# Four graph layers on one core: another fold in the convolution, hub blocks loaded earlier, messages kept in SBUF, a last chunk by tiles

## The chip, the cores and the metric

The kernel runs on one core of a Trainium2 chip, as one launch. The metric is the device time of that launch in microseconds. The engines are named as the profile names them: PE is TensorE's matrix products and PEld its weight loads, DVE is VectorE, ACT is ScalarE, POOL is GpSimd, and SP is SyncE, whose queue issues most of the DMAs.

## The reference

`x` has 8 graphs of 2048 nodes with 64 features, and `adj` (2048 x 2048, ones and zeros) is one graph's edges, shared by all eight. Node numbers near zero have many neighbours (the probability of an edge falls with the root of each end's number). Four layers follow one another, each as `x = x + layer(relu(layernorm(x)))`:

```python
# layer 0: attention over hyperedges, mixed with a product adj @ (x W_ind)
pair = jnp.stack([industry, g], axis=2)
coefs2 = softmax(tanh(pair @ fcW + fcb) @ av, axis=-1)
out = einsum('bnk,bnkf->bnf', coefs2, pair)

# layer 1: a Chebyshev graph convolution with weights of each node
w = einsum('nd,dkio->nkio', embedding, weight)      # K = 3 orders, 16 embedding numbers
As = [I, A, 2 A A - I]
x_g = einsum('knm,bmc->bnkc', stack(As), x)
out = einsum('bnki,nkio->bno', x_g, w) + b

# layer 2: three steps of message passing
for _ in range(3):
    effects = einsum('nm,bmd->bnd', adj, v)
    h = relu(concat([v, effects]) @ W1.T + b1)
    v = h @ W2.T + b2

# layer 3: graph attention over adj, softmax, h_prime + bias
```

So the adjacency is multiplied into something five times after layer 0: twice for the Chebyshev orders of layer 1, and once in each step of layer 2.

## The kernel before

**Layout.** The 2048 nodes are 16 tiles of 128 (`NT`), four tiles are a chunk of 512 (`TC`, `CW`), and there are four chunks (`NC`). The 8 x 64 features are four pairs q of 128 (`NP`: two graphs by 64 features). Tensors are held transposed, features on the partitions, in two `Halves`; slots of SBUF named `q0` to `q9` are handed from stage to stage by their names. Messages, with nodes on the partitions (128 x 512 a tile, 256 KB), go to DRAM as `sent[...]`.

**The product with adj.** For a target tile t the first three source tiles (`HUBS` = 3) are dense: six products of 128x512 from a copy in two parts (`Hub`, high and low). The other sources of t are a list of rows; each group of up to 128 is gathered from `sent` by an indirect DMA on POOL (`Feed.fetch`, L2578), split in two parts by ACT (L2595) and DVE (L2596), and multiplied with a 128x128 block of adj (`cells`). `LISTED` says how many groups a tile has: 7, 6, 5, 4 or 3. Target 0 is different: it takes all 13 other tiles whole (`FAR` = 13, blocks `zero`), which SP loads from `sent` (L2576). `Feed` keeps `raws` gathered tiles and splits `ahead` of the products; `group` is how many blocks of weights one cast on ACT covers. `Feed.own` loads the target's own message for the diagonal term, and `finish` makes z.

**The mixing (`mix`, L686).** The last stage of layer 0, chunk by chunk, with `Lists.fill` (L2472) beside it: 60 indirect DMAs bring blocks of adj and DVE masks them into `cells`.

**First product of layer 1 (`layer1_near`, L1624).** `Lists.load` (L2506) loads the three dense rows of blocks (1 MB each) and the 13 blocks of target 0, each cast on DVE to bf16. Then 16 targets; each result goes to DRAM as `sent[1]`.

**Convolution (`convolution_near`, L1679).** The second order is a product with adj again, made chunk by chunk by the generator `product(place)`, one chunk ahead of the convolution that uses it; `product(0)` runs alone before the convolution begins. The convolution of a chunk runs over the four pairs q and over blocks of the embedding, two at a time; for each block PE makes four products with `w01` (both first orders) into one of six PSUM banks `pk`, then, with `w2`, adds the second order; DVE multiplies the bank by the embedding's row (L1834), and POOL adds it to one of two accumulators `half` (L1840; the last block's add is DVE's). Each accumulator holds two halves of 64 partitions, of which the sum over halves is the result. `fold_up` lets PE add the halves with a stationary matrix `fold` into the bank `side`, and DVE adds that to x (L1736). `waiting` is a list of small pieces of work (fold, norm, store, messages) that are popped once after each pair of blocks (twice in the last chunk), and `advance()` spreads the pieces of the next product evenly over 30 places. Messages of the first step of layer 2 are made here in the last chunk; `send` (L1864) copies each from PSUM to `u` and stores it.

**Layer 2 (`layer2_near`, L1880).** Three steps of 16 targets. After each target, `turn` transposes z and applies ReLU, and `after` either makes the next step's message or, in step 2, at the end of each chunk, runs `chunk`: product with `w2`, residual, norm (`Scores.chunk`, L2726: centre, squares, root, reciprocal L287, write), the first products of layer 3, and their rows to DRAM (`f_rows`, L2753). Beside the steps a generator `neighbours` (L1975) sorts the lists for layer 3 with MAX8 and MATCH_REPLACE on DVE, one instruction per group of products. `Scores` is made at the start of layer 2, with its small loads and a product of `aa`.

**Layer 3** gathers from `f_rows` on POOL (L2819), and its result ends the kernel.

The order on each engine is that of the program as a scheduler moved it; engines run their own queue in order.

Of the kernel before, what the change touches and what calls it, by code (L numbers as in the profile page):

```python
# [19 lines left out]
P = 128  # L20
# [26 lines left out]
F16 = mybir.dt.float16  # L47

# [86 lines left out]
class Kernel:  # L135
# [1488 lines left out]
    def layer1_near(self, slots, k2, far):  # L1624
# [11 lines left out]
        with (  # L1636
# [3 lines left out]
            lists.load(w)  # L1640
# [38 lines left out]
    def convolution_near(self, slots, k):  # L1679
# [27 lines left out]
        fold = k.tile([P, D], F, name="fold")  # L1707
        nc.vector.tensor_add(fold, ident[:, lo], ident[:, hi])

        with (  # L1710
# [21 lines left out]
            def fold_up(q, accs):  # L1732
                po = side()
                for i, h in enumerate((lo, hi)):
                    self.mm(po[h], fold, accs[i])
                nc.vector.tensor_add(x[:, q], po, x[:, q])  # L1736

            def message(t):
                pn = steps.first_message(v, t, bank())
                self.send(0, t, pn, lists.hub, w)  # L1740

            feed = Feed(
                self, lists, w, self.sent[1], None, raws=4, casts=2, ahead=1, group=2,
# [3 lines left out]
            def product(place):  # L1747
                ch, aah = chunks[place], aahs[place % 2]

# [7 lines left out]
                for i in range(TC):  # L1757
                    t = ch * TC + i
                    own = feed.own(t)
                    acc = ps.tile([P, CW], F, name="acc")  # L1760
                    feed.dense(acc, t, lists.hub)
                    yield
                    for n, _ in enumerate(feed.listed(acc, t)):
                        if n == 1 and last is not None:
                            turn(*last)
                        yield
# [18 lines left out]
            def pieces(place):  # L1785
                targets = [chunks[place] * TC + i for i in range(TC)]
                return sum(2 + (LISTED[t] or FAR) for t in targets)

# [6 lines left out]
            for place, ch in enumerate(chunks):  # L1795
# [4 lines left out]
                many, hook = 0 if ends else pieces(place + 1), 0  # L1800

                def advance():
                    nonlocal hook
                    for _ in range(many * hook // 30, many * (hook + 1) // 30):
                        next(ahead, None)
                    hook += 1

                if ends:
                    for c in chunks[:-1]:
                        for t in range(c * TC, (c + 1) * TC):  # L1810
                            waiting.append(lambda t=t: message(t))
                for q in range(NP):
                    accs = [w.tile([P, CW], F, name="half", bufs=4) for _ in range(2)]
                    sides = list(enumerate(((xe, hi), (xo, lo))))
                    for blk in range(0, NBLK, 2):
# [7 lines left out]
                        advance()  # L1823
# [19 lines left out]
                        advance()  # L1843
                        if waiting:
                            waiting.pop(0)()
                    waiting[:0] = [lambda: None, lambda q=q, accs=accs: fold_up(q, accs)]
# [3 lines left out]
                norm = self.norm_parts(ch, x, Part(v, s), Part(u, s), std, bank, write)  # L1850
# [13 lines left out]
    def send(self, step, t, pn, hub, w, later=None):  # L1864

        nc = self.nc
        u = w.tile([P, CW], F, name="u", tag="z")
# [12 lines left out]
    def layer2_near(self, slots, k2):  # L1880
# [3 lines left out]
        with (  # L1884
# [9 lines left out]
            last = Scores(self, slots, k, w, ps)  # L1894
            accs, late = {}, []

            def messages(step, t):
                pn = ps.tile([P, NP, P], F, name="pn")
                for q in range(NP):
                    self.mm(pn[:, q], v(q)[:, t * P : (t + 1) * P], seen[step])  # L1900
                self.send(
                    step, t, pn.rearrange("n q f -> n (q f)"), hubs[step], w, later[:, 2]
# [22 lines left out]
            def chunk(ch):  # L1925
                s = slice(ch * CW, (ch + 1) * CW)
                x = last.x
                nc.sync.dma_start(x, self.xs[2][ch])
                for q in range(NP):
                    p2 = ps.tile([P, CW], F, name="p2")  # L1930
# [4 lines left out]
                self.store_x(2, ch, x)  # L1935
                last.chunk(ch)

            def after(step, t):
                if step < 2:
                    messages(step + 1, t)  # L1940
                elif t % TC == TC - 1:
                    chunk(t // TC)
# [4 lines left out]
            for step in range(3):  # L1947
# [3 lines left out]
                feed = Feed(self, lists, w, self.sent[2 + step], None)  # L1951
                for t in range(NT):
                    own = feed.own(t)
# [418 lines left out]
class Lists:  # L2372
# [99 lines left out]
    def fill(self, pool, w):  # L2472
# [3 lines left out]
        self.cells = pool.tile([P, PLACE[NT], P], BF, name="cells")  # L2476
# [8 lines left out]
        for c in range(0, PLACE[NT], group):  # L2485
# [8 lines left out]
            if len(late) > 2:  # L2494
                keep(*late.pop(0))
            yield
        for x in late:
            keep(*x)
        yield

    def open(self, pool):
        self.dense = pool.tile([P, HUBS, N], BF, name="dense")
        self.zero = pool.tile([P, FAR, P], BF, name="zero")
        self.hub = Hub(pool, "hub")

    def load(self, w):  # L2506

        nc, a = self.nc, self.kern.a
        for h in range(HUBS):
            raw = w.tile([P, N], F, name="dense_raw", bufs=1)  # L2510
            nc.sync.dma_start(raw, a["adjT"][h * P : (h + 1) * P])
            nc.vector.tensor_copy(self.dense[:, h], raw)
        raw = w.tile([P, FAR, P], F, name="zero_raw", bufs=1)
        nc.sync.dma_start(
            raw, a["adjT"][HUBS * P :, :P].rearrange("(i p) n -> p i n", p=P)
        )
        nc.vector.tensor_copy(self.zero, raw)
# [177 lines left out]
class Scores:  # L2695
# [3 lines left out]
    def __init__(self, kern, slots, k, w, ps):  # L2699
# [6 lines left out]
        self.sums = k.tile([P, NP, NC], F, name="sums")  # L2706
# [19 lines left out]
    def chunk(self, ch):  # L2726
        nc, kern = self.nc, self.kern

        def write(q, ch, xr, scale):
            nc.vector.scalar_tensor_tensor(  # L2730
                self.hn[:, q], xr, 1.0, scale, op0=OP.mult, op1=OP.mult,
                accum_out=self.sums[:, q, ch : ch + 1],
            )

        std = self.w.tile([P, CW], F, name="std", bufs=1)
# [394 lines left out]
```

## Time and profile before

The times are of nine runs; the profile is of one more execution. The mean clock granted to TensorE is a share of full speed.

| what | value |
|---|---|
| time, median of 9 runs | 1979.48 us |
| lowest and highest | 1972.14 and 1984.28 us |
| the profiled execution: its time | 1980.55 us |
| the profiled execution: span | 1978.8 us, mean clock 0.908 |
| PE busy | 1699.3 us, 86% |
| DVE busy | 1410.7 us, 71% |
| ACT busy | 810.8 us, 41% |
| POOL busy | 1035.3 us, 52% |
| gathers L2578 on POOL | 300, 1053 ns each |
| loads of own messages from `sent` (SP) | 52 of 256 KB, 4.2 us to landing |
| loads of whole messages for target 0 (SP) | 52 of 256 KB, 3.3 us to landing |
| stores of messages (SP) | 48 of 256 KB, 3.5 us to landing |

Stages in the profiled execution, in us from the start of the span: layer 0 to 621, of it the mixing from 479; the first product of layer 1 to 738; `product(0)` to 786; the convolution to 1253; its end, with norm and messages, to 1297; layer 2's steps to 1669, where step 0's last z is at 1406.92 and step 1's at 1528.34; the last chunk of layer 2 to 1702; layer 3 to the end. A row of a group gives the line, the engine, the operation, what it writes and reads, shapes and count; then its busy time and the mean of one in ns; then the idle time of the engine before it, and who ended that idle time.

### The profile page before, as it was taken

How to read it: one execution, taken by the hardware profiler on the slowest of the kernel's cores; microseconds unless marked ns; L12 is line 12 of the kernel's file. 1: busy time of each engine (PE TensorE's matmuls, PEld its weight loads, DVE VectorE, ACT ScalarE, POOL GpSimd, SP SyncE). 2: the span in 40 equal slices, each digit the busy share in tenths (PEclk: the TensorE clock that was granted, in tenths of full speed). 3: DMA queues.
4: the chain of work that ended last, by engine and by line, in shares of the span. 5: the costliest groups of instructions: out<-in, count | busy, mean ns of one | idle time of the engine just before them, and what ended most of it. 6: DMA issues, size and time to landing. Idle time of an engine off the chain costs nothing. (4 is left out here: it accounts for less than half of the span.)

```text
span 1978.8 us, 22332 instructions
## 1 busy us (share of the span) xinstructions
PE 1699.3 (86%) x7061; PEld 973.8 (49%) x7066; DVE 1410.7 (71%) x2389; ACT 810.8 (41%) x1627; POOL 1035.3 (52%) x959
## 2 busy tenths in 40 slices
PE   6859798998996787999999999769888899579885
PEld 2515666665323564444444444447667565345432
DVE  6777778885667674877677657588988576459774
ACT  5712354554664663222121010255666664257300
POOL 1100166666870753876765645266474641478770
PEclk8867899998996888999999989789989999789887
DMA  9740223344335776333131210368788774666665
GB/s 349 257 120 1 72 75 103 106 129 176 105 101 175 232 229 183 85 85 112 49 109 40 65 52 38 108 218 246 238 266 271 218 260 160 230 180 174 183 178 191
DMA packets 124057, 305.20 MB, mean 154 GB/s; under 512 B 29312, under 2 KB 31120, under 8 KB 118160
## 3 DMA queue, kind: packets, MB, share of 16 engines
q0 software_dynamic: 45328, 149.60, 25.1%
q1 hardware_dynamic: 76288, 149.80, 22.7%
q10 hardware_dynamic: 2304, 4.20, 0.6%
q8 instruction: 59, 0.97, 0.2%
q14 instruction: 78, 0.64, 0.1%
HBM read 240.40 MB, written 63.14 MB: 153 GB/s over the span
## 5 line engine op out<-in xcount | busy, mean ns | idle before, releaser
L2578 POOL DMA_INDIRECT raw<-sent,index x300 | 315.8, 1053 | 306.0 <-DVE part_lo L2596 119.9
L2596 DVE TENSOR_TENSOR part_lo<-raw,part_hi 128x512 fp32r<-128x512 f32 x352 | 265.6, 777 | 120.1 <-ACT part_hi L2595 106.0
L2595 ACT CAST part_hi<-raw 128x512 fp32r<-128x512 f32 x352 | 212.4, 619 | 314.8 <-PE acc L176 208.6
L1840 POOL TENSOR_TENSOR half<-half,y 128x512 f32<-128x512 f32 x192 | 247.3, 1317 | 133.9 <-DVE y L1834 128.7
L176 PE MATMUL pk<-q,w 128*128 128x512 f32 (+1 forms) x768 | 301.4, 610 | 2.4 <-DVE q L1724 0.9
L176 PE MATMUL acc<-q,ident 128*128 128x512 f32 x416 | 202.6, 613 | 24.6 <-DVE q L2909 18.2
L176 PE MATMUL acc<-part_hi,weights 128*128 128x512 f32 x365 | 176.0, 485 | 30.4 <-ACT part_hi L2595 30.0
L1834 DVE SCALAR_TENSOR_TENSOR y<-pk,bias,q 128x512 f32<-128x512 f32 x224 | 158.0, 742 | 52.2 <-PE pk L176 32.9
L176 PEld LDWEIGHTS pk<-q,w 128*128 128x128 f32 (+1 forms) x768 | 115.7, 190 | 155.9 <-issue 119.8
L176 PE MATMUL acc<-part_lo,weights 128*128 128x512 f32 x365 | 166.7, 458 | 24.5 <-DVE part_lo L2596 23.9
L2819 POOL DMA_INDIRECT ring<-f_rows,near x121 | 142.0, 1173 | 65.0 <-issue 28.9
L176 PEld LDWEIGHTS acc<-q,ident 128*128 128x128 f32 x416 | 76.9, 194 | 98.2 <-issue 43.0
L2305 POOL TENSOR_TENSOR q<-q,beta 128x512 f32<-128x512 f32 x57 | 76.1, 1337 | 72.4 <-DVE beta L2281 33.8
L176 PEld LDWEIGHTS acc<-part_hi,weights 128*128 128x128 f32 x365 | 74.2, 203 | 80.9 <-ACT part_hi L2595 46.9
L176 PEld LDWEIGHTS acc<-part_lo,weights 128*128 128x128 f32 x365 | 74.0, 203 | 72.7 <-DVE part_lo L2596 56.1
L176 PE MATMUL pp<-adj,x_ind_hi 128*128 128x512 f32 x256 | 89.3, 464 | 0.5 <-DVE q L846 0.3
L2564 ACT CAST hub_weights<-dense 128x384 fp32r<-128x384 bf16 x80 | 40.6, 511 | 101.4 <-PE acc L176 97.2
L2890 DVE TENSOR_TENSOR q<-ring,e 128x1024 f32<-128x1024 f32 x58 | 70.1, 1219 | 8.4 <-PE acc L176 8.2
L2305 POOL TENSOR_TENSOR q<-q,coef 128x512 f32<-128x512 f32 x57 | 63.1, 1108 | 20.9 <-DVE q L2328 17.6
L176 PE MATMUL pp<-adj,x_ind_lo 128*128 128x512 f32 x256 | 72.7, 404 | 0.0
L287 DVE RECIPROCAL std<-std 128x512 f32<-128x512 f32 x16 | 53.6, 3351 | 25.9 <-ACT std L286 21.9
L2489 POOL DMA_INDIRECT listed_raw<-in_adjT_dram,cell x60 | 62.9, 1048 | 16.5 <-issue 15.9
(503 smaller groups left out, 3427.6 us busy)
## 6 DMA issues: line engine op xcount, KB each, us to landing
rows<-in_adj_dram SPq DMA_DIRECT2D x16, 1024.0 KB, 9.1
adj_t<-in_adjT_dram SPq DMA_DIRECT2D x64, 256.0 KB, 3.0
own<-sent SPq DMA_DIRECT2D x52, 256.0 KB, 4.2
raw<-sent SPq DMA_DIRECT2D x52, 256.0 KB, 3.3
sent<-u SPq DMA_DIRECT2D x48, 256.0 KB, 3.5
q<-x SPq DMA_DIRECT2D x10, 1024.0 KB, 5.4
x<-q SPq DMA_DIRECT2D x9, 1024.0 KB, 3.9
links<-squares POOLq DMA_DIRECT2D x16, 512.0 KB, 8.2
```

Of the source, the lines that this page charges most:

```text
L176: self.nc.tensor.matmul(out, lhsT, rhs, start=start, stop=stop)
L287: nc.vector.reciprocal(std, std)
L1834: nc.vector.scalar_tensor_tensor(y, pks[b, half], bias[:, b : b + 1], emb[:, b], op0=OP.add, op1=OP.mult,)
L1840: add.tensor_add(acc, acc, y)
L2305: self.nc.gpsimd.tensor_tensor(x, x, by.unsqueeze(2).to_broadcast([P, NB, D]), op=OP.mult)
L2489: self.kern.behind(nc.gpsimd.indirect_dma_start(raw[:, i], None, rows, bass.IndirectOffsetOnAxis(ap=self.cell[:, c + i : c + i + 1], axis= ...
L2564: self.nc.scalar.copy(to, self.lists.dense[:, :, i * P : (i + 1) * P])
L2578: self.nc.gpsimd.indirect_dma_start(raw, None, self.rows[:], bass.IndirectOffsetOnAxis(ap=self.lists.index[:, c : c + 1], axis=0),)
L2595: nc.scalar.copy(hi, raw)
L2596: nc.vector.tensor_sub(lo, raw, hi.bitcast(F))
L2819: self.nc.gpsimd.indirect_dma_start(to, None, self.kern.f_rows[:], bass.IndirectOffsetOnAxis(ap=index, axis=0))
L2890: nc.vector.tensor_tensor(y.rearrange("n i (b f) -> n i b f", b=NB), block[:, i : i + 2, : NB * D].rearrange("n i (b f) -> n i b f", b=NB) ...
```

## The change

- The lists of blocks (`cells`, `dense`, `zero`) are held in unsigned 8-bit numbers, no longer in bf16. `Lists.load` is gone: `bring` loads the dense blocks and those of target 0 in 16 pieces (256 KB, the last one 64 KB) and casts each on DVE, one piece per step of `fill`, beside the mixing.
- `product(0)` takes four of the six `pk` banks as accumulators and makes all its hub products first. The feed of the convolution has `ahead` 3 for 1 and `group` 4 for 2; `own` has two buffers for one. `advance()` and its 30 places are gone: the next product goes on once for every second pair of blocks, a target being cut in two parts (target 0 in four).
- The sum of the halves: no `fold` product. `cross` copies the two half-accumulators that lie on the wrong partitions into `other` by two DMAs inside SBUF, and `fold_up` makes two adds of 64x512 and one of 128x512 on DVE, all in SBUF.
- In steps 0 and 1 of layer 2 the messages stay in SBUF (`kept`, the slots q2 and q3) as well as going to `sent`: `own` and the 13 tiles of target 0 are read from there. In the convolution's last chunk, the message of each chunk's last tile is made later than the others, and squares of the last norm lie in another buffer.
- The feed of layer 2 has `raws` 8 for 6 and `ahead` 4 for 2. `Scores` is made at the start of step 2.
- In step 2 the last four tiles go through `chunk` one at a time, 128 wide; x for layer 3 is stored in slices of the chunk.

```diff
@@ -1637,7 +1638,6 @@
-            lists.load(w)
             hub = Hub(w, "first_hub")
@@ -1729,23 +1726,39 @@
-            def fold_up(q, accs):
-                po = side()
+            def cross(accs):
+                other = w.tile([P, CW], F, name="other", bufs=1)
+                nc.sync.dma_start(other[lo], accs[0][hi])
+                nc.sync.dma_start(other[hi], accs[1][lo])
+                return other
+
+            def fold_up(q, accs, other):
                 for i, h in enumerate((lo, hi)):
-                    self.mm(po[h], fold, accs[i])
-                nc.vector.tensor_add(x[:, q], po, x[:, q])
+                    nc.vector.tensor_add(x[h, q], accs[i][h], x[h, q])
+                nc.vector.tensor_add(x[:, q], other, x[:, q])
+
+            kept = Halves(slots, "u", ("q2", "q3"), True)
 
             def message(t):
                 pn = steps.first_message(v, t, bank())
-                self.send(0, t, pn, lists.hub, w)
+                self.send(0, t, pn, lists.hub, kept(t))
 
             feed = Feed(
-                self, lists, w, self.sent[1], None, raws=4, casts=2, ahead=1, group=2,
+                self, lists, w, self.sent[1], None, raws=4, casts=2, ahead=3,
                 targets=[ch * TC + i for ch in chunks for i in range(TC)],
             )
 
             def product(place):
                 ch, aah = chunks[place], aahs[place % 2]
+                sums = {}
+
+                def begin(t):
+                    sums[t] = bank() if place == 0 else ps.tile([P, CW], F, name="acc")
+                    feed.dense(sums[t], t, lists.hub)
+
+                if place == 0:
+                    for i in range(TC):
+                        begin(ch * TC + i)
@@ -1757,13 +1770,15 @@
                     own = feed.own(t)
-                    acc = ps.tile([P, CW], F, name="acc")
-                    feed.dense(acc, t, lists.hub)
-                    yield
+                    if place > 0:
+                        begin(t)
+                    acc = sums.pop(t)
+                    stops = [LISTED[t] // 2 - 1] if t else [2, 6, 9]
                     for n, _ in enumerate(feed.listed(acc, t)):
-                        if n == 1 and last is not None:
+                        if n in stops:
+                            yield
+                        if n == stops[0] and last is not None:
                             turn(*last)
-                        yield
@@ -1797,17 +1808,9 @@
-                many, hook = 0 if ends else pieces(place + 1), 0
-
-                def advance():
-                    nonlocal hook
-                    for _ in range(many * hook // 30, many * (hook + 1) // 30):
-                        next(ahead, None)
-                    hook += 1
-
@@ -1820,7 +1823,8 @@
-                        advance()
+                        if blk % 4 == 0 or (q == 0 and chunks[(place + 1) % NC] == 0):
+                            next(ahead, None)
@@ -1840,14 +1844,19 @@
-                        advance()
                         if waiting:
                             waiting.pop(0)()
-                    waiting[:0] = [lambda: None, lambda q=q, accs=accs: fold_up(q, accs)]
+                    waiting[:0] = [
+                        lambda: None,
+                        lambda q=q, accs=accs, other=cross(accs): fold_up(q, accs, other),
+                    ]
+                    if ends and q < NP - 1:
+                        waiting.append(lambda t=q * TC + TC - 1: message(t))
@@ -1922,24 +1931,28 @@
-            def chunk(ch):
-                s = slice(ch * CW, (ch + 1) * CW)
-                x = last.x
-                nc.sync.dma_start(x, self.xs[2][ch])
+            def chunk(t, n):
+                ch, c = t // TC, t % TC * P
+                s = slice(t * P, t * P + n)
+                x = last.x[:, :, c : c + n]
+                if c == 0:
+                    nc.sync.dma_start(last.x, self.xs[2][ch])
...
             def after(step, t):
                 if step < 2:
                     messages(step + 1, t)
+                elif t >= NT - TC:
+                    chunk(t, P)
                 elif t % TC == TC - 1:
-                    chunk(t // TC)
+                    chunk(t - TC + 1, CW)
@@ -1948,9 +1961,12 @@
-                feed = Feed(self, lists, w, self.sent[2 + step], None)
+                    last = Scores(self, slots, k, w, ps)
+                feed = Feed(
+                    self, lists, w, self.sent[2 + step], kept if step < 2 else None, raws=8, ahead=4
+                )
                 for t in range(NT):
-                    own = feed.own(t)
+                    own = kept(t) if step < 2 else feed.own(t)
@@ -2473,7 +2489,10 @@
-        self.cells = pool.tile([P, PLACE[NT], P], BF, name="cells")
+        self.cells = pool.tile([P, PLACE[NT], P], U8, name="cells")
+        self.dense = pool.tile([P, HUBS, N], U8, name="dense")
+        self.zero = pool.tile([P, FAR, P], U8, name="zero")
+        dense = self.bring(w)
@@ -2493,28 +2512,41 @@
+            next(dense, None)
             yield
...
+    def bring(self, w):
+
+        for src, to in self.blocks():
+            raw = w.tile([P, 4, P], F, name="dense_raw", bufs=2)
+            raw = raw[:, : src.shape[1]] if len(src.shape) == 3 else (
+                raw.rearrange("p i n -> p (i n)")
+            )
+            self.nc.sync.dma_start(raw, src)
+            self.nc.vector.tensor_copy(to, raw)
+            yield
```

`Halves` is the class that the features already use: two tiles in named slots, here indexed by node tile.

## The prediction

> **What bounds the kernel now.** I read the busy times by stage first, since the page's chain of waits holds only 1% of the span and names nothing in the stages that the change touches. Columns: window, its length, then busy time of each engine with instruction count, the granted TensorE clock, DMA share, GB/s.
>
> ```profile
> core 0: us, PE busy (x) PEld busy (x) DVE busy (x) ACT busy (x) POOL busy (x), PEclk, DMA share, GB/s
> 479.00:621.00 142.00, 121.55 (x417) 40.56 (x415) 91.45 (x120) 77.23 (x107) 96.46 (x92) 0.89 0.40 128
> 738.00:786.00 48.00, 34.26 (x102) 20.35 (x103) 20.76 (x33) 18.71 (x40) 16.97 (x16) 0.77 0.66 197
> 786.00:1253.00 467.00, 459.17 (x1476) 196.92 (x1475) 327.26 (x433) 72.56 (x142) 293.51 (x240) 0.99 0.22 69
> 1253.00:1297.00 44.00, 32.20 (x116) 19.80 (x114) 25.20 (x42) 18.27 (x34) 5.89 (x6) 0.77 0.55 183
> 1297.00:1340.00 43.00, 29.02 (x144) 22.31 (x144) 36.65 (x52) 24.34 (x48) 28.51 (x27) 0.82 0.66 200
> 1340.00:1410.00 70.00, 65.87 (x391) 54.76 (x391) 63.33 (x83) 42.19 (x86) 39.54 (x37) 0.97 0.82 259
> 1410.00:1425.00 15.00, 10.92 (x46) 7.53 (x45) 14.73 (x19) 8.69 (x16) 4.80 (x4) 0.90 0.69 229
> 1425.00:1530.00 105.00, 92.10 (x504) 73.48 (x504) 88.81 (x119) 65.50 (x131) 68.52 (x65) 0.93 0.84 265
> 1530.00:1546.00 16.00, 13.99 (x64) 9.94 (x62) 12.28 (x19) 10.04 (x19) 4.72 (x5) 0.89 0.71 219
> 1546.00:1640.00 94.00, 88.79 (x426) 58.54 (x426) 63.35 (x112) 60.00 (x123) 52.19 (x52) 1.00 0.73 233
> ```
>
> The convolution (786 to 1253) is TensorE's: 459 of 467 us busy at a clock of 0.99, VectorE 327, GpSimd 294. The stretch before it, its own first product, is not: 34 busy of 48. In layer 2, PE and DVE are both nearly full in steps 0 and 1 (DVE 14.73 of 15 in the first change of step); step 2 is PE's.
>
> Then the groups of the convolution, shapes apart (count, busy us, mean ns, idle before and its releasers):
>
> ```profile
> L2596 DVE TENSOR_TENSOR part_lo<-raw,part_hi 128x512 fp32r<-128x512 f32 x55 | 68.5, 1256 | 31.2 <-ACT part_hi L2595 31.2
> L176 PE MATMUL side<-half,fold 128*64 128x512 f32 x62 | 17.6, 624 | 3.5 <-DVE half L1840 3.5
> L1736 DVE TENSOR_TENSOR q<-side,q 128x512 f32<-128x512 f32 x15 | 10.2, 678 | 0.0
> ```
>
> The product that folds two half accumulators is 17.6 us of a full engine. DVE's split L2596 takes 1256 ns here; the same shape in layer 2 takes 688:
>
> ```profile
> L2596 DVE TENSOR_TENSOR part_lo<-raw,part_hi 128x512 fp32r<-128x512 f32 x196 | 129.3, 688 | 45.8 <-ACT part_hi L2595 36.2 <-PE acc L176 7.8 <-ACT q L1920 1.0
> ```
>
> Last, single waits in the order of time (start, us, what, idle before in brackets), and the sum of waits over layer 2's steps (us, times, longest):
>
> ```profile
> 637.12 0.79 PE L176 MATMUL acc<-first_hub_h,hub_weights 128*128 128x512 f32 x1 [4.29 <-ACT hub_weights L2564]
> 741.51 0.94 POOL L2578 DMA_INDIRECT raw<-sent,index  x1 [11.46 <-PE acc L176]
> 748.45 0.62 ACT L2595 CAST part_hi<-raw 128x512 fp32r<-128x512 f32 x1 [5.37 <-DMA raw<-sent,index]
> 1290.10 1.01 POOL L2578 DMA_INDIRECT raw<-sent,index  x1 [34.18 <-DMA raw<-sent]
> POOL raw L2578 <- DMA raw<-sent: 30.4, 2, 20.0
> ```
>
> Gathers at the start of layer 2 wait for plain loads of the messages that target 0 needs in full; so they do at both changes of step.
>
> **The change, part by part.** All against the profiled execution, 1980.55 us (span 1978.8), 1.1 above the median of the runs shown.
>
> A, hub blocks in the mixing. Removed after 621: three casts L2512 of 1.23 and one of 1.02 on DVE, and SP's 1 MB loads between the stores; PE's first hub product waits 4.29 at 637. Gain 4.29, up to 10 if the first gather (643.81) follows: I take −6. Added in the mixing: 16 loads of 256 KB and 16 casts to 8 bits. That cast is in no row; bounds are a quarter of the 1.23 cast (0.31) and the 0.69 of other 128x512 passes, so 5 to 11 us of DVE. In the built order they stand in the first one and a half chunks of the mixing, where DVE is 20 to 21 busy of 35 us. Each waits at DVE's head for its landing (3.0 us in the row of the 256 KB adj_t loads), with L759 to L761 queued behind, which PE's products of the mixing await. Two buffers hide about half. If the 14 idle us per 35 cover all, 0; otherwise 12. I take +6. A together: 0 (−10 to +12).
>
> B, first product. Gathers take 1.25 us apart when not held (741.51, 742.76, 744.01); before, they are held by split buffers up to 6.8 us, and one accumulator serialises the four targets until 786. Four banks put all 24 hub products ahead of the data, and splits go four deep. Sixteen gathers × 1.25 = 20 us from 741.5, plus 7 from issue to first split, plus 4 for last split, products, z and turn: 772 to 774 instead of 786: −13 (−8 to −16, the latter if all follow A's earlier start).
>
> C, convolution. Off PE: −17.6, and of the 3.5 us idle ahead of it nothing counted. Onto DVE: three adds with both inputs in SBUF for one of 0.68, 16 times: 3 × 0.69 − 0.68 = 1.4 alone, or 3 × 1.256 − 0.68 = 3.1 at the stretch the split shows; 22 to 50 us of DVE, hidden by its 140 idle. If that cover is gone, up to +50 less the 17.6. Onto SP: 32 copies of 128 KB inside SBUF; the nearest row is 3.3 us for 256 KB. They wait at SP's head for the halves, with own rows, messages' stores and embedding loads behind; the add stands two hooks (some 11 us) later, so nothing waits, save after the last quarter: there copy 3.3 + adds 2.1 stand for products 1.3 + add 0.7, +3.4. The thirty small interruptions become eight lumps per chunk; I give them +1. C: −13 (−21 to +8).
>
> The Trainium skill, "SBUF — State Buffer", section "Who interferes with whom", speaks against the three adds: a VectorE instruction with both inputs in SBUF and a GpSimd instruction that reads SBUF exclude each other for whole instructions. The row agrees in kind (1256 against 688). By the rule at its worst each add waits out one GpSimd add of 1.317 us, 16 × 3 × 1.32 = 63 us of DVE, still under its 140 idle, so the time would be the same; by the row it is 27.
>
> D, messages kept on chip. At layer 2's start 13 loads L2576 issued over 1277.5 to 1289.1 go; the last message's store is issued by 1274.35 and takes 3.5, so gathers can begin at 1278 instead of 1290. DVE and PE have room (25 and 32 of 44), yet t=0 must still be split 13 times: −9 (−5 to −12). The small loads for the scores and PE's 3.49 wait on them move to step 2, hidden by PE's queue of ready products; no gain counted.
>
> At the changes of step, z of target 15 to z of target 0 takes 18.5 (1406.92 to 1425.40) and 17.3. Loads vanish there, and splits go four deep in place of two (E). But DVE is full there with the neighbour sort (MAX8 2.29, MATCH_REPLACE 2.27), and a wait removed only brings its next work forward. Over 1297 to 1546 DVE is busy 215.8 of 249 and PE 211.9: no more than 33 can go. The fullest long stretch now has PE at 94% (65.87 of 70), so I take half: −16 (0 to −30). Step 2 is at 88.79 of 94: −2 (0 to −5). DMA share there is 0.82 to 0.84, and 52 own and raw loads fewer only help.
>
> F, last chunk by tiles. Today's tail from the last z (1669.24) to the first gather of layer 3 (1702.01) is 33 us: turn 2.0, product p with its add to 1676, centring and squares to 1680.4, root to 1682.3, reciprocal 3.35, back and writes to 1692, four tiles' stores to 1699.5, then 2.5. At a quarter of the wide parts the last tile's own chain is 2.0 + 1.2 + 1.1 + 1.2 + 0.8 + 1.6 + 1.9 + 2.5 = 12.3; the tiles that queue before it after the last listed product, a chain and a half at some 8, make it 25. But all four have serial links on PE's in-order queue: small products waiting for ACT and DVE stop listed products behind them. Tail −8, stalls +5: −3 (−8 to +6).
>
> Sum: 0 − 13 − 13 − 9 − 16 − 2 − 3 = −56: 1924.5, less 1.1 for the median: 1923.
>
> **Rivals.** R1: layer 2 is DVE's. The sort and the splits only close ranks; the changes of step, deeper splits and tiles give nothing: −13 −13 −9 = −35, 1944. For it: 14.73 of 15 at the first change, 36.65 of 43 at the start. Against: 16 us of DVE idle in 1425 to 1530, and part_hi waiting for DMA 41.6 us.
>
> R2: the convolution turns to DVE/GpSimd locally; −13 becomes +5: 1941. For: the stretch above. Against: 140 idle us.
>
> R3, slower: the lumps. Three products ahead × 8 lumps; each brings up to four gathers in a row on GpSimd, which holds them until split buffers come free (longest 4.7 us in the convolution now, 38.8 in 26 waits), and its adds of y queue behind; y has three buffers, so DVE stops, then the six banks fill and PE stops. At 24 × 3 = 72 us the time is 1995. It decides from 24 × 2.6 = 62, my 56 and the 6 that tell a difference. Against: six banks hold one and a half pairs of blocks, each pair 5.6 us of PE, more than the longest hold.
>
> R4: it does not do what it says: loads in the mixing hold DVE for 3.0 + 0.69 each without overlap, 59 us in all, while the rest gains: 1923 + 53 = 1976. Against: the order has them in pairs with two buffers.
>
> **How the numbers follow.** Forecast 0.52, R1 0.22, R2 0.10, R3 0.08, R4 0.03, and 0.05 that more is won in layer 2 (33 of 33, below 1905). About 6 us (0.3%) can be told from none. Faster: all but R3, nearly all of R4 and an edge of R2: 0.88; within: 0.03; slower: 0.09. The forecast's own range is 1900 to 1946, its terms' half-widths combined; 1892 to 1958 takes in R1, R2 and some of the deeper gain, and leaves out R3 and R4.
>
> **What would show it.** A: first hub product near 630 and DVE waits on dense loads in 479 to 560 of some 6 us. B: from the first gather to the convolution's steady state about 32 instead of 45. C: no side<-half rows, PE still 97% busy, the stretch 13 shorter; L1737-like adds of 0.7 to 1.3. R3 shows as PE idle by DVE y in lumps. D: first gather of layer 2 some 4 us after the last store. E: changes of step near 12 to 14, DVE over 92%; if DVE is at 88% and the changes still 17, R1. F: last z to first gather near 25. The forecast is wrong if GpSimd, with gathers and adds in one queue, sets the pace anywhere in 786 to 1253.

## The result, and the profile after

The changed kernel takes 2002.6 us (median of 10 runs, 1988.85 to 2009.95); beside it the kernel before has 1978.07 (31 runs). The ratio is 1.011, with an interval from 1.009 to 1.013: slower by some 22 us, where 56 less were forecast. Run again in a later call it was 1.0121 (1.0089 to 1.0152).

The profiled execution of the changed kernel has a span of 2000.0, 21.2 above that of before. Cut at events that both kernels have, the difference lies as follows (us; "again" are profiles of the same two kernels from one later call):

| stage, from event to event | before | after | difference | before again | after again |
|---|---|---|---|---|---|
| start to the mixing's reciprocal at 556 (before) | 556.4 | 563.1 | +6.7 | 550.9 | 560.6 |
| to the last target of the first product, stored on its way | 181.6 | 178.3 | -3.3 | 184.4 | 177.1 |
| product(0), to its last z | 45.7 | 36.8 | -8.9 | 45.9 | 38.2 |
| convolution, to the reciprocal of its last chunk | 476.4 | 490.1 | +13.7 | 476.6 | 489.5 |
| to layer 2's first z | 37.3 | 25.5 | -11.8 | 38.2 | 25.1 |
| step 0, to its last z | 109.6 | 112.6 | +3.0 | 105.7 | 112.9 |
| step 1 | 121.4 | 121.3 | -0.1 | 123.2 | 123.0 |
| step 2, to the z of target 14 | 131.1 | 134.9 | +3.8 | 131.5 | 136.5 |
| to the z of target 15 | 9.8 | 15.7 | +5.9 | 9.8 | 15.7 |
| to layer 3's first gather | 32.8 | 40.3 | +7.6 | 33.2 | 40.1 |
| layer 3 | 276.8 | 281.4 | +4.6 | 279.1 | 276.7 |

The signs repeat in the second pair, except in layer 3, whose own code is the same in both kernels; step 1, which the change does touch, took the same time in both pairs. Two stages lost what the sum wanted to gain: the convolution, and the end of layer 2.

The windows of the changed kernel, which answer to those of before (window, length, then busy time and count of each engine, clock, DMA share, GB/s):

```profile
core 0: us, PE busy (x) PEld busy (x) DVE busy (x) ACT busy (x) POOL busy (x), PEclk, DMA share, GB/s
479.00:628.00 149.00, 122.84 (x410) 41.13 (x411) 95.41 (x129) 78.79 (x110) 92.51 (x90) 0.86 0.41 130
742.00:780.00 38.00, 31.26 (x105) 20.72 (x106) 20.00 (x32) 19.47 (x36) 16.56 (x16) 0.81 0.82 245
780.00:1262.00 482.00, 452.02 (x1413) 194.34 (x1411) 344.99 (x467) 69.02 (x129) 285.96 (x239) 0.98 0.25 75
...
1340.00:1406.00 66.00, 57.79 (x340) 49.16 (x340) 61.81 (x81) 38.31 (x78) 39.71 (x32) 0.95 0.59 178
1406.00:1425.00 19.00, 15.32 (x80) 11.46 (x78) 16.72 (x23) 11.32 (x24) 7.07 (x8) 0.92 0.43 133
1425.00:1528.00 103.00, 87.00 (x488) 73.85 (x489) 87.94 (x118) 63.49 (x129) 68.68 (x62) 0.93 0.81 254
1528.00:1548.00 20.00, 16.36 (x81) 12.46 (x80) 13.98 (x25) 11.18 (x22) 5.76 (x5) 0.92 0.49 144
```

In the convolution PE has less to do (452 busy) and yet the stage is longer: its idle time grew from 8 us in 467 to 30 in 482. In step 0 DVE is now busy 61.81 of 66, more densely than PE. The rows at 1406 and 1528 are the two changes of step: z of target 15 to z of target 0 takes 17.9 and 18.5 now, 18.5 and 17.3 before.

Groups of the convolution (count, busy, mean ns of one, idle before and its releasers) show who holds PE up. The first line is the kernel before, the others are the changed kernel:

```profile
L176 PE MATMUL pk<-q,w 128*128 128x512 f32 x500 | 231.7, 603 | 2.0 <-DVE q L1724 0.9 <-DVE y L1834 0.7
...
L177 PE MATMUL pk<-q,w 128*128 128x512 f32 x502 | 242.8, 620 | 23.1 <-DVE half L1838 10.8 <-DVE y L1838 8.1 <-DVE q L1721 2.1
...
L1737 DVE TENSOR_TENSOR q<-half,q 64x512 f32<-64x512 f32 x32 | 21.8, 681 | 0.5
...
L1738 DVE TENSOR_TENSOR q<-other,q 128x512 f32<-128x512 f32 x15 | 10.9, 726 | 21.7 <-DMA other<-half 19.8 <-issue 1.8
```

PE's products into `pk` waited 2.0 us in all before, 23.1 now, for banks that DVE has not read. And DVE stands 19.8 us for the copies of the fold. One quarter in order of time (start, us, what, idle before):

```profile
813.67 0.52 SPq L1731 DMA_DIRECT2D other<-half  x1
...
814.17 1.40 DVE L1737 TENSOR_TENSOR q<-half,q 64x512 f32<-64x512 f32 x2
814.28 0.56 SPq L1732 DMA_DIRECT2D other<-half  x1
818.19 0.69 DVE L1738 TENSOR_TENSOR q<-other,q 128x512 f32<-128x512 f32 x1 [2.62 <-DMA other<-half]
...
820.01 0.74 DVE L1838 SCALAR_TENSOR_TENSOR half<-pk,bias,q 128x512 f32<-128x512 f32 x1
...
820.81 9.18 PE L177 MATMUL pk<-q,w 128*128 128x512 f32 x20 [3.07 <-DVE half L1838]
```

The copies are issued at 813.7 and 814.3; the add that needs them is DVE's next work but one, and waits 2.62 us; behind it queue two splits and the next pair's first multiplication, and PE waits 3.07 for that. The program writes this add eight multiplications later. The scheduler had moved it up, and the order of the built kernel already said so.

The waits of layer 2's steps (us, times, longest) have lost the row of target 0's plain loads, and the first two that remain are about as large as before. The first two lines are the kernel before, the others the changed kernel, both from 1300 to 1640:

```profile
POOL raw L2578 <- DVE part_lo L2596: 56.9, 43, 6.8
ACT part_hi L2595 <- DMA raw<-sent,index: 41.6, 44, 2.9
...
POOL raw L2610 <- DVE part_lo L2628: 53.7, 22, 27.0
ACT part_hi L2627 <- DMA raw<-sent,index: 47.3, 46, 3.1
```

At the end of layer 2 the chains by tiles run one after the other (timelines, cut to the steps that repeat; the first line is the one wide reciprocal of the kernel before, the others are the changed kernel):

```profile
1682.31 3.35 DVE L287 RECIPROCAL std<-std 128x512 f32<-128x512 f32 x1 [1.96 <-ACT std L286]
...
1678.31 0.73 DVE L2671 SCALAR_TENSOR_TENSOR z<-own,self_weight,acc 128x512 f32<-128x512 f32 x1
...
1682.85 0.95 DVE L288 RECIPROCAL std<-std 128x128 f32<-128x128 f32 x1 [1.11 <-ACT std L287]
...
1688.39 2.30 PE L177 MATMUL p<-q,w 128*128 128x128 f32 x8
...
1694.35 0.95 DVE L288 RECIPROCAL std<-std 128x128 f32<-128x128 f32 x1 [1.02 <-ACT std L287]
...
1700.20 2.30 PE L177 MATMUL p<-q,w 128*128 128x128 f32 x8
...
1706.69 0.95 DVE L288 RECIPROCAL std<-std 128x128 f32<-128x128 f32 x1 [1.25 <-ACT std L287]
...
1718.66 0.94 POOL L2857 DMA_INDIRECT ring<-f_rows,near  x1 [15.43 <-DVE own L2963]
```

The reciprocals of tiles 13, 14 and 15 lie 11.5 and 12.3 us apart. A tile's first products `p` stand in PE's queue behind the last products of the tile before, so nothing of one chain covers the other. The 512-wide chain had one reciprocal of 3.35; three of 0.95 are no longer, but the waits from one engine to the next, such as DVE's 1.02 to 1.25 us in front of each reciprocal, are paid three times after the last z.

### The profile page after: what moved, and what is told of

The parts are those of the page before. It is cut to its first block, busy times and chain, and to the rows that moved or that the text cites. A ratio compares the mean times of both kernels' runs of the same rounds, so it can differ in the third digit from the quotient of the medians.

```text
span 2000.0 us, 22470 instructions
## 1 busy us (share of the span) xinstructions
PE 1688.5 (84%) x7093; PEld 982.0 (49%) x7098; DVE 1431.0 (72%) x2477; ACT 808.0 (40%) x1629; POOL 1036.0 (52%) x959
## 3 DMA queue, kind: packets, MB, share of 16 engines
q1 hardware_dynamic: 74672, 140.37, 21.2%
## 5 line engine op out<-in xcount | busy, mean ns | idle before, releaser
L2610 POOL DMA_INDIRECT raw<-sent,index x300 | 325.1, 1084 | 300.2 <-DVE part_lo L2628 148.1
L177 PE MATMUL pk<-q,w 128*128 128x512 f32 (+1 forms) x768 | 310.7, 623 | 23.1 <-DVE half L1838 10.8
L2628 DVE TENSOR_TENSOR part_lo<-raw,part_hi 128x512 fp32r<-128x512 f32 x326 | 244.1, 776 | 87.7 <-ACT part_hi L2627 81.9
L1844 POOL TENSOR_TENSOR half<-half,y 128x512 f32<-128x512 f32 x192 | 241.1, 1284 | 119.3 <-DVE y L1838 118.3
L2627 ACT CAST part_hi<-raw 128x512 fp32r<-128x512 f32 x326 | 195.4, 619 | 195.5 <-DMA raw<-sent,index 88.1
L177 PE MATMUL acc<-part_hi,weights 128*128 128x512 f32 x349 | 156.5, 450 | 26.1 <-ACT part_hi L2627 25.5
L177 PE MATMUL acc<-part_lo,weights 128*128 128x512 f32 x349 | 155.0, 446 | 16.8 <-DVE part_lo L2628 16.5
L177 PEld LDWEIGHTS acc<-part_hi,weights 128*128 128x128 f32 x349 | 69.1, 198 | 51.6 <-ACT part_hi L2627 39.1
L2596 ACT CAST hub_weights<-dense 128x384 fp32r<-128x384 uint8 x80 | 40.6, 510 | 105.3 <-PE acc L177 102.3
L288 DVE RECIPROCAL std<-std 128x512 f32<-128x512 f32 (+1 forms) x19 | 54.1, 2847 | 33.8 <-ACT std L287 33.8
L2321 POOL TENSOR_TENSOR q<-q,coef 128x512 f32<-128x512 f32 x57 | 63.0, 1106 | 21.0 <-DVE q L2344 17.6
```

Source lines behind the costliest of these rows:

```text
L177: self.nc.tensor.matmul(out, lhsT, rhs, start=start, stop=stop)
L288: nc.vector.reciprocal(std, std)
L1844: add.tensor_add(acc, acc, y)
L2321: self.nc.gpsimd.tensor_tensor(x, x, by.unsqueeze(2).to_broadcast([P, NB, D]), op=OP.mult)
L2596: self.nc.scalar.copy(to, self.lists.dense[:, :, i * P : (i + 1) * P])
L2610: self.nc.gpsimd.indirect_dma_start(raw, None, self.rows[:], bass.IndirectOffsetOnAxis(ap=self.lists.index[:, c : c + 1], axis=0),)
```

## The experiments

Calls differ: in the call of the first four runs, and in that of the last three, the kernel before took 2026.5 us, and step 1 of layer 2 took 124 to 139 us in their profiles. Totals are therefore told as ratios to the kernel before in the same call. Stages are in part set beside those of another call. The convolution bears that: it took 490.1 and 489.5 in two profiles of the changed kernel and 476.4 and 476.6 in two of the kernel before. Layer 2 and layer 3 don't, where one of the two calls took 2026.5.

**The last chunk whole.**

```diff
-                elif t >= NT - TC:
-                    chunk(t, P)
```

> The last chunk of layer 2 goes as one again, 512 wide; all else as in the changed kernel (2002.6 us). Theory: four chains by tiles, one after another in PE's in-order queue at 12 us each, are what made the end of layer 2 late (last z 6 us later than the target before it, then 40.3 us to layer 3's first gather instead of 32.8): 13 us less, 1987 to 1992, and the first gather of layer 3 33 us after the last z. Rival: the last z is late for the deeper splits of step 2 and layer 3 starts slowly for its own reasons: 5 us less at most, 1997 to 2003.

Measured 1.0072 (1.0043 to 1.0101): target 14 to target 15 took 11.9 instead of 15.7, and last z to first gather 33.0 instead of 40.3. The theory's stage times hold; 11 us belong to the tiles. (The ratio alone falls just short of the expected one, and the changed kernel had not run in that call.)

**The fold's adds held where the program writes them.**

```diff
-                    nc.vector.tensor_add(x[h, q], accs[i][h], x[h, q])
-                nc.vector.tensor_add(x[:, q], other, x[:, q])
+                    self.behind(nc.vector.tensor_add(x[h, q], accs[i][h], x[h, q]))
+                self.behind(nc.vector.tensor_add(x[:, q], other, x[:, q]))
```

> The three adds of the fold are held in DVE's order where the program writes them, eight multiplications later; all else as in the changed kernel (2002.6 us). Theory: the scheduler had put them directly behind the last add of the halves, so DVE stood at its head for the copy (19.8 us in 12 waits) and PE for DVE's banks; held back, the copies have landed: waits on the copy under 3 us, and 10 to 15 us less, 1987 to 1993. Rival: the convolution lost its time to the lumps of the next product and to contention between DVE and GpSimd: the waits go, the time stays within 4 us of 2002.

Measured 1.0116 (1.007 to 1.0161). The convolution took 477.0 instead of 490.1, as the theory says, and DVE waited for no copy; the total showed no gain, as the rival says, but the changed kernel had not run in that call, where layer 2 took longer in every run, so the total decided nothing yet. It did show a new cost: the adds took 1346 and 1232 ns in the mean in place of 681 and 726.

**The fold on PE again.** `cross` and the SBUF adds go, `fold` and `side` return as before.

> The fold is PE's product again, no copies and one add from PSUM; all else as in the changed kernel (2002.6 us). Theory: PE gets 17.3 us of work back and loses the waits on the copy (some 13) and part of the idle that is left: 1999 to 2006, no gain. Rival: three adds in SBUF against GpSimd's adds are the cost beside the wait: 1985 to 1993.

Measured 1.012 (1.0072 to 1.0167); the convolution 479.4. PE's 19.0 us of folding are paid by the waits that left (PE waits 9.6 us for `pk`, not 23.1). The theory holds; in the convolution the change's fold and the old one were worth the same once no copy was waited for.

**The next product in thirty pieces again.** `advance()` and the old yields return; the rest stays.

> The next product is spread over 30 places again, piece by piece, with the copies and adds of the fold, four banks and deeper splits as in the changed kernel (2002.6 us). Theory: the lumps are a smaller part of the convolution's loss of 13.8 us against the kernel before: 3 to 7 us less, 1995 to 2000. Rival: the lumps are all of it, DVE and GpSimd standing in blocks for splits: 13 us less or more, 1980 to 1990.

Measured 1.0144 (1.0097 to 1.0192), convolution 488.9. Both expectations fell: going back to pieces gained nothing here.

**On one chip, with the kernels themselves beside.** Four runs of one call.

> The kernel before, for a profile from the chip on which the next three run. Chips differ: the first four experiments ran where the kernel before took 2026.5 us, not 1978. Every theory expects the stages of the first profile (181.6 us first product, 45.7 product(0), 476.4 convolution, 37.3 its end, 109.6, 121.4 and 131.1 the steps, 32.8 from last z to first gather), the convolution within 3 us, the steps up to 20 us longer on a slow chip.

> The changed kernel, timed on the same chip as the next two. If the loss belongs to the kernel and not to the chip, 1.008 to 1.015 times the kernel before; the convolution 490, last z to first gather 40.

These two are the columns "again" of the table above: every stage of before within 5.5 us of the first profile, and the changed kernel at 1.0121, with 489.5 and 40.1.

> Two edits together on the changed kernel: adds of the fold held eight multiplications later, and the last chunk whole. Theory: the two losses are apart in time and add: 13 us from the convolution (490 to 477) and 11 to 13 from the end (56 to 45 from the target before the last to the first gather), 22 to 27 us less than the changed kernel, so 0.997 to 1.002 times the kernel before. Rival: what is won in the convolution is given back in layer 2 (its stages were as slow or slower in the run with late adds): 8 to 13 us less, 1.004 to 1.008.

Measured 0.9993 (0.9972 to 1.0014): 0.0128 under the changed kernel's ratio in the same call, some 25 us (23 by the medians). Convolution 477.2, target 14 to first gather 44.8 instead of 55.8. The two losses are apart and add; without them the kernel takes as long as the one before the change. Groups of the convolution in this run:

```profile
L1737 DVE TENSOR_TENSOR q<-half,q 64x512 f32<-64x512 f32 x32 | 43.1, 1346 | 0.5
...
L1738 DVE TENSOR_TENSOR q<-other,q 128x512 f32<-128x512 f32 x16 | 19.7, 1232 | 0.5
```

No wait, but 1346 ns for an add that took 681 in the changed kernel. Held later, the adds run while GpSimd adds `half` (1338 ns each in this run): 30 of the 32 overlap such an add in time and take 1391 ns in the mean, the two that don't take 683. DVE's time for the fold is then 62.8 us, against 10.2 for the one add from PSUM before.

> The two edits, and the next product spread over 30 places again. Theory: with the copies landed, DVE is what PE waits for in the convolution (adds of 1.64 us beside GpSimd, blocks of splits), and evenly spread splits free it: convolution 465 to 472, 0.991 to 0.997 times the kernel before. Rival: GpSimd's port, not the lumps, sets DVE's pace: convolution 476 to 480, no difference to the kernel with two edits.

Measured 1.0021 (0.9998 to 1.0045), convolution 485.9. The theory fell, and the rival too: with the adds held later, pieces are 9 us worse than lumps. The traces show where that can come from: PE's products of `part_hi` take 444 ns each in lumps (24.9 us busy in the convolution of the run before this one) and 616 in pieces (34.5). The same is seen in the run with pieces above (636 ns) and in the kernel before (615). The lumps so saved PE some 10 us, which the forecast had not counted; no run isolates it.

**Which part of the fold costs: copies, or adds.** Two runs of one call, both with the last chunk whole.

> Last chunk whole. The two copies of each fold are left out, so the halves on the other partitions are missing from the sum: the third add reads a tile of zeros, cleared once; DVE's adds, their count and their place directly behind the halves stay as in the changed kernel. Theory: the convolution's 490 hold 20 us of DVE waiting for copies; without them and with adds that run beside no GpSimd add (0.69 each) it is 466 to 472. Rival: DVE's three adds themselves hold PE up: 476 or more.

Measured 0.9982 (0.9965 to 0.9998), convolution 471.7: near the upper edge of the theory. Without the wait, 18 us of the 490 are gone, though DVE does the same adds.

```diff
+                                if b == 0 and half == 1 and folds:
+                                    folds.pop(0)()
                                 if b > 0:
...
+                    other = cross(accs)
+                    fold_up(q, accs)
+                    if q < NP - 1:
+                        folds.append(lambda q=q, other=other: fold_in(q, other))
```

> Last chunk whole; the two adds of 64 partitions stay directly behind the halves, the third, of the copied part, is held until the next pair's first two multiplications are done, before GpSimd's next adds begin. Theory: adds of 0.69 us instead of 1.23 to 1.35 beside GpSimd, and a wait on the copy of at most 1 us: convolution 468 to 474, 0.994 to 0.998 times the kernel before. Rival: the copy takes longer than the place gives it, DVE waits as in the changed kernel: 480 or more, 1.001 to 1.006.

Measured 0.9911 (0.9888 to 0.9935), convolution 464.6, better than the theory had both. Its groups:

```profile
L177 PE MATMUL pk<-q,w 128*128 128x512 f32 x504 | 236.7, 608 | 8.3 <-DVE y L1841 7.3 <-DVE half L1841 0.4
...
L1737 DVE TENSOR_TENSOR q<-half,q 64x512 f32<-64x512 f32 x32 | 21.8, 681 | 0.5
...
L1740 DVE TENSOR_TENSOR q<-other,q 128x512 f32<-128x512 f32 x16 | 12.3, 767 | 1.8 <-issue 1.2 <-DMA other<-half 0.4 <-DVE q L282 0.2
```

The add comes after the two multiplications that PE waits for and before GpSimd's next adds, so it hardly waits for the copy (0.4 us in all), and 13 of the 16 share no time with GpSimd's adds (682 ns each; the other three 1135). PE's wait for banks is 8.3 us instead of 23.1. It beats the run without any copy by 7 us; there the third add still stands in front of those two multiplications, and PE waits 13.7 for banks.

**The hub blocks, and layer 2's feed**, each undone on top of the run at 0.9993. The first puts `lists.load(w)` back before the first product; the second drops `raws=8, ahead=4`.

> Adds held later, last chunk whole (0.9993 times the kernel before), and the hub blocks loaded after the mixing again, in 8 bits. Theory: loading them in the mixing costs it 7 to 10 us and gives the first product 5 back: mixing's end at 554 to 557 instead of 564, first product 182, 2 to 6 us less. Rival: mixing is as long without the loads, the difference of 7 to 10 us is the 8-bit lists: no change in the mixing, 4 us more in the first product.

Measured 0.9967 (0.9951 to 0.9982): the mixing's event at 552.8 against 565.2, the first product 185.3 against 178.0. The theory holds, and its net is some 5 us; the ratio's interval overlaps that of 0.9993, so the size rests on the stages, 12.4 us less and 7.3 more. In the changed kernel the casts of the dense blocks read (ns least, median, most; then idle time ahead of them):

```profile
L2548 DVE CAST dense<-dense_raw x12: 412/427/1780, 484.5 to 515.4; 128x512 uint8<-128x512 f32 x12
...
its engine sat idle before it (us, times) until:
  DMA dense_raw<-in_adjT_dram: 16.6, 10
```

A cast is 0.43, and DVE stands 16.6 us for landings.

> Adds held later, last chunk whole, and layer 2's feed with 6 gathered tiles and splits two deep again. Theory: DVE and PE full in steps 0 and 1, so depth gives nothing: steps within 3 us of 107.5, 123.0, 133.8. Rival: depth is a gain that the messages kept on chip hide: 5 to 15 us longer over the three steps.

Measured 0.9946 (0.9924 to 0.9968): steps 111.3, 120.0 and 128.7, the last z 10.1 after that, against 107.5, 123.0, 133.8 and 11.9. Neither expectation: shallow is 6 us better over the steps and some 9 by the ratio. Depth is a small loss, most of it in step 2, and its size is rough: the three other runs of this call, with the deep feed and the last chunk whole, took 3 to 13 us longer than this one over the same stages.

**Do the four add up, and what gave the gains.**

> Four edits on the changed kernel: last chunk whole, third add after the halves, hub blocks loaded after the mixing, layer 2's feed 6 tiles and two splits deep. Theory: the gains lie in different stages and add: from 0.9911 (two of them) another 0.0026 for the hub blocks and 0.003 to 0.005 for the feed: 0.983 to 0.988 times the kernel before; convolution 465, first product 185, steps 111, 120, 129. Rival: layer 2's feed and the earlier start give the same time twice: 0.989 to 0.992.

Measured 0.9824 (0.9779 to 0.9869), 1994.66 against 2026.51 in that call. The gains add as the theory says (the total is just under its range of 0.983 to 0.988), and the convolution took 464.6 again; the first product took 186.3 and the steps 111.5, 123.8 and 143.2, of which step 2 is far from the 129 expected. This version beats the kernel before in that call. It did not run in a call where the kernel before takes 1978, so how much it gains there is not shown; the run with two of the four edits had 0.9911 in such a call.

> As the run with four edits, but steps 0 and 1 of layer 2 load their own messages and target 0's thirteen from DRAM again (the messages still lie in SBUF as well). Theory: the end of the convolution to target 0's z goes from 26 to 37 us, and each change of step loses at most 2, since DVE is full there: 9 to 15 us more. Rival: loads at changes of step cost what they seemed to, 5 us each, too: 18 to 25 us more.

Measured 0.9864 (0.9814 to 0.9915), 11 us above it. Layer 2's first z came 30.4 after the convolution's reciprocal instead of 26.1, steps 0 and 1 took 4.7 and 8.7 longer. The change of step from 0 to 1 took 18.3 instead of 15.4. The 11 us are what the theory said, but by its stages most of it lies in the steps; the intervals of the two ratios overlap, so the size stays rough. The expected 37 was wrong: some 7 of the 12 us at the start of layer 2 do not come from reading messages in SBUF. Which of the other edits there gave them (scores made later, the order of the messages) was not tried.

> As the run with four edits, but the convolution's feed splits one deep and casts weights in groups of two, as before; four banks stay. Theory: the four banks give product(0) little without the depth, since each gather waits for a split buffer: product(0) 43 to 46 instead of 37. Rival: banks give it: 36 to 39. The rest of the convolution within 3 us of 465 by both.

Measured 0.9865 (0.9821 to 0.9909). product(0) took 39.4 against 37.8: the rival is right, four banks give its gain. But the convolution took 473.6 against 464.6: both expected no difference. So the deeper splits and the wider casts together are worth 9 us there. How is not shown: the run takes back both at once, and PE does not wait longer for banks in it (1.9 us against 7.9) but is busy longer (461.9 us against 448.2).

## Why the prediction was wrong

**The convolution (-13 forecast, +13.7).** The saving on PE came, but smaller: the 17.6 us of `side` products are gone, and yet its busy time fell by only 7 in the window (459 to 452), and by 11 in the run with the moved add (448 of 464); the products into `pk` took 242.8 and 236.7 us there, 231.7 before. The step that failed is "the add stands two hooks (some 11 us) later, so nothing waits". That is the program's order, not DVE's. On DVE the add stood directly behind the halves and waited 19.8 us in all, though a copy took 2.2 us from issue to landing in the median (2.2 to 4.7 in the trace), less than the 3.3 that the forecast took; meanwhile DVE emptied none of PE's six banks, and PE waited. The second failed step is "hidden by its 140 idle": DVE's price for the fold, 22 to 50 us by my bounds, was 44 to 53 above the old add, with the wait or with GpSimd beside it, and it fell between a bank's filling and its reading, where PE waits. A mean over a stage says nothing about that. The rival R2 named the place and gave it +5; it was mis-sized by 9.

**GpSimd beside DVE.** The forecast drew on the Trainium skill, "SBUF — State Buffer", section "Who interferes with whom": a VectorE instruction with both inputs in SBUF excludes a GpSimd instruction that reads SBUF. The runs agree: the same add took 681 ns away from GpSimd's adds and 1346 in the mean where 30 of 32 overlap them. By the forecast's own reckoning DVE's idle time would hide that; the runs show that what it costs depends on where in DVE's queue the add stands.

**The last chunk (-3 forecast, +13.5).** The step that failed is "a chain and a half at some 8": after the last z it was nearly three chains, 12 us each. The links at a quarter width were sized well enough (a reciprocal of 0.95 against 0.8), but each chain also waits from engine to engine (1.02 to 1.25 us before a reciprocal), and PE's queue holds one tile's products behind the other's.

**Layer 2's steps (-18 forecast, +6.7).** The steps that failed are "Loads vanish there" and "I take half" of the 33 us. Loads vanish only at the first change of step: the changed kernel reads kept messages in steps 0 and 1 alone, and step 2 still loads its 13 tiles from `sent`, so the second change could not gain by it (18.5, before 17.3). At the first one the loads are gone, but it took 17.9 instead of the 12 to 14 forecast: DVE is busy 16.72 of 19 us there, which is the forecast's own sign for R1 (88%, changes still 17). At the second DVE is busy 13.98 of 20, so a full DVE doesn't explain that one. R1, which gave these steps nothing, was nearer than the forecast. "Half" followed from no row, as PE at 94% says nothing of DVE, which was at 14.73 of 15. The run with the shallow feed puts the deeper splits at some 6 us of loss, and its changes of step took 16.4 and 16.6.

**What held.** The mixing's +6 was +6.7 from the start of the span, partly by luck: layer 0 came to the mixing 3.6 us earlier in that profile, and from its last reciprocal before the mixing on the two kernels differ by 10.2 (8.4 in the second pair). DVE's waits on dense loads were 16.6, not some 6. The first product's -6 was -3.3; undone, the pair is worth some 5 us, so A cost 5 where 0 was forecast, within the stated -10 to +12. PE's first hub product lost its wait but came at 636.8, not near 630: the mixing ended 6.7 later, and PE's transposes behind it, which had ended at 632.8, now run to 636.9. product(0) went from first gather to last z in 33 us, near the forecast (32), but the 45 that this was set against ran to 786, some 2 us behind the last z; from first gather to last z it was 42, so 9 us were gained and not 13. The start of layer 2 gave 11.8 for 9, though not all by the reason given. R3, the one rival on the slower side, named the lumps; going back to pieces gained nothing, and with the adds held later the lumps are 9 us better.

So the forecast missed mainly by three terms: the convolution by 27 us, layer 2's steps by 25, the last chunk by 17. In the first and the last the order on an engine's queue was taken from the program or guessed, and not read; without these two losses the kernel takes as long as before, and is still far from the 56 us of gain.

## What to carry to other kernels

When work moves from a full engine to one with idle time, look where on that engine's own queue the scheduler puts it, and what stands behind it: an add that waits for a DMA at the head of DVE's queue stopped PE here, and with the same add behind two multiplications PE's wait for banks fell from 23.1 to 8.3 us. A wide chain cut into tiles only gains if the tiles overlap; check in each engine's order that a tile's first link stands ahead of the last link of the tile before. And a change of several parts is best judged part by part: here the place of an add, the chains by tiles, the early hub blocks and the deep feed of layer 2 cost some 25, 11, 5 and 6 us and hid what the rest gains. Without them the same change ran at 0.982 times the kernel before, in a call where that took 2026.5 us.

## What was not expected of the hardware

Calls differ more than the edits do: the kernel before took 1978 to 1983 us in three calls and 2026.5 in two, and in the latter step 1 of layer 2 was 124 to 139 us in nearly the same kernel, instead of 120 to 124. The chip alone doesn't explain it: by the chip's number noted with the runs, four runs with 1978.1 for the kernel before and, in a later call, three with 2026.5 were on the same one. The work is the same and the waits are longer: in layer 3, whose code these runs share, PE is busy 209.0 us and DVE 179.3 in the run with the shallow feed, where the stage takes 280.0, and 210.1 and 179.8 in the run with four edits, where it takes 297.6. What the engines wait for there, and why in some calls, is open. A ratio from one such call and a stage from another must not be mixed.
